# In the last two context blocks a pair's zero-point terms are written while the pair in front of it is multiplied

## The chip, the cores and the metric

The kernel runs on one core of one Trainium2 chip. The metric is the device time of one execution in microseconds, the median of several runs. The engines are called as the profile calls them: PE (TensorE, matmuls), PEld (its weight loads), ACT (ScalarE), DVE (VectorE), POOL (GpSimd) and SP (SyncE, which issues most DMAs).

## The reference

Two layers are computed for x (2 x 1024 x 2048) and a context ctx (2 x 2048 x 2048), all in float32. The first is a quantised product with the context, the second a feed-forward product with low-rank additions:

```python
def fake_quant(x, scale, zp):
    q = jnp.clip(jnp.round(x / s + z), 0.0, 255.0)
    return (q - z) * s
x = x + matmul(fake_quant(layernorm(x), x1_scale, x1_zp), fake_quant(ctx, x2_scale, x2_zp))
z = layernorm(x)                      # seen as 8 groups of 256 rows, one gate row each
delta = B_eff(gate) @ (A_eff(gate) @ z) + B_shared @ (A_shared @ z)
x = x + z @ kernel + bias + delta     # A_eff, B_eff: gated sums over 16 low-rank pairs
```

## The kernel before

**Batches, groups and blocks.** The two batches b run one after the other. The 1024 rows of a batch are four groups g of 256 rows, each of which is two tiles of 128 rows, j = 0 and 1. The 2048 columns of the context are four blocks n of 512. The quantised rows (`c1T`, less 128) and the quantised context block (`c2`, less 128) are small whole numbers and are multiplied in bf16. What is still missing from the product because the zero point is not 128 is added as two terms: `colt[n]`, a row of 512 values that belongs to the block, and `r_s`, a value for each row.

**A pair.** One group with one block is a `Pair` (line 513). Its accumulator `pa` is a tile of two PSUM banks, one for each j. Three such tiles, with the tags acc0, acc1 and delta, are used in turn, so that a pair takes the tile of the pair three before it. For each j, `begin(j)` (line 523) lets ScalarE write `colt + r_s` into the bank, and `products(j, ...)` (line 528) adds 16 matmuls of 128x128 by 128x512 to it. Then `end()` (line 545) lets VectorE scale both banks and add them to y, and `stats()` (line 549) takes the statistics for the second layer norm. `late(j)` (line 540) adds the terms afterwards instead; three early pairs of batch 0 use it.

**The order of the pairs.** In batch 0 all pairs of blocks 0 and 1, and pair (n=2, g=0), run in `entry()` by the list `STEPS`, an order written out by hand, which also keeps VectorE, ScalarE and PE in that order. The rest of batch 0, and all pairs of batch 1, go through `xattn_pair` (line 555). Pairs are named (n, g) below. The loops that call it for the last two blocks are those of lines 1056 and 1071. Beside the pairs of block 2 they round and centre block 3 of the context (`quantise`, lines 458 and 464), make the gated sums of the first low-rank factor (`lora_a_step`, line 593: matmuls of line 574 into `pg_a`, a copy of line 590, transposes of line 600, copies of line 606) and then block 3's column term (`column_term`, line 474: matmuls of lines 486 and 505, and line 511 that writes `colt`). Beside the pairs of block 3 they make the gated sums of the second factor (`lora_b_step`, line 611: line 574 into `pg_b`, a copy of line 590, and small DMAs of line 616 on SP's queue), load the first weights of the feed-forward part, and normalise and transpose each group that is complete (`group_z`, line 635: VectorE's line 628, PE's transposes of line 632 into `ptz`, ScalarE's copies of line 633). After pair (3,2) and group 1 `lora_ax` (line 642) multiplies the first two groups with the low-rank factor (`px`, line 648), and VectorE adds the halves of two groups (line 1093), two of them into buffers that a gated sum has read. The feed-forward products follow (line 828, `fu`, `fv`, `fw`), a scheme with seven products of sums of quarters (lines 31 to 50), whose operands VectorE and GpSimd combine (lines 762 and 771).

**Rows prepared between pairs.** In batch 0 all row tiles are prepared in `entry()`. In batch 1 the tiles of groups 0 and 1 are prepared during the feed-forward part of batch 0, and those of groups 2 and 3 (tiles 4 to 7) between the pairs of blocks 0 and 1, by the loop of lines 1036 to 1041: `prep_x` for both tiles of a group, then the group's pairs with blocks 0 and 1. The preparation (`prep_x`, line 436) takes VectorE's statistics, ScalarE's rounding of the row (line 409), and then for each half of the row ScalarE's centring with a running sum (line 412), eight transposes on PE (line 423) and VectorE's copy into `c1T` (line 428). At the end VectorE makes the tile's `r_s` from the two sums (line 432). The centred half rows have one buffer each (`qh`, two halves in the scratch tile `wk`), which all row tiles share, so a tile's line 412 follows the transposes of the tile before it.

**What sets the order.** Outside `entry()`, the order of the instructions on each engine is worked out when the kernel is built, from a model of their durations: of the instructions whose inputs the model says are there, the one that was written first in the program goes first. `tc.high_priority()` puts what it encloses in front of others that are ready. On the chip each engine then works through its list in that order, and waits where an input is late.

In `xattn_pair` the begin of the second half is written behind the products of the first half:

```python
for j in range(MG):
    with tc.high_priority():
        p.begin(j)
    p.products(j, range(KT))
```

Of the kernel before, what the change touches and what calls it, by code (L numbers as in the profile page):

```python
# [98 lines left out]
def tile_quant_xattn_then_lora_ffn(  # L99
# [27 lines left out]
    GPB = GB // B  # L127
    GT = B * S // GB
    MG = GT // P
# [38 lines left out]
    def bf(t, n):  # L168

        return t.rearrange("p k n -> p (k n)").bitcast(BF16).rearrange("p (k n) -> p k n", n=n)  # L170
# [280 lines left out]
    def quantise(c2, r):  # L451

        centre_ctx(c2, r, round_ctx())
# [20 lines left out]
    def column_term(b, n, c2):  # L474

        of = column_parts(b, n, c2)
        column_copy(of)
        column_mean(b, n, of)
        column_end(n, of)
# [72 lines left out]
                    st2[:, self.g * MG + j, self.n, :], y[self.g][:, j, ds(self.n * NB, NB)]  # L552
                )

    def xattn_pair(b, n, g, c1T, c2):
        p = Pair(b, n, g, c1T, c2)
        for j in range(MG):
            with tc.high_priority():
                p.begin(j)
            p.products(j, range(KT))  # L560
        summed = p.end()
        p.stats()
        return summed
# [29 lines left out]
    def lora_a_step(b, n):  # L593

        lora_a_place(n, lora_a_turn(b, n, *gated(f"a{b}_{n}")))
# [15 lines left out]
    def lora_b_step(b, n):  # L611

        st, sf = gated(f"b{b}_{n}")
        for c in range(NC):
            for i in range(2):
                nc.sync.dma_start(
                    out=bd[b][i::2, i, ds(c * RC, RC), ds(n * NB, NB)],
                    in_=sf[ds(c * GP + i * (GP // 2), GP // 2), :],
                )
        q2b.give(st)  # L620
# [14 lines left out]
    def group_z(b, g, wk, zq):  # L635
        for j in range(MG):
            prep_z(b, g * MG + j, zq, wk)
        for q in range(4):
            nc.scalar.dma_start(out=zs[b][g][q], in_=zq[q])
        return zq  # L640

    def lora_ax(b, pr, zqs):

        px = ps_m.tile([P, GT], F32, tag="pm", name=f"px_{b}_{pr}")
        for k in range(KT):
            for i in range(2):
                g = 2 * pr + i
                nc.tensor.matmul(  # L648
                    px[i * 2 * R : (i + 1) * 2 * R, :],
                    acat[:, k, ds(3 * pr + i, 2), :].rearrange("p s r -> p (s r)"),  # L650
                    zqs[i][k // KQ][:, k % KQ, :],
                    start=(k == 0),
                    stop=(k == KT - 1),
                    skip_group_check=True,
                )
        nc.scalar.copy(axT[:, pr, :], px)
# [245 lines left out]
    c1T = [bf(t, GT) for t in c1T_bufs]  # L902
    wk = big.take()
    c2b = {}
    c2 = {}
# [114 lines left out]
    for b in range(B):  # L1020
        if b == 0:
            open_c2(0)
            open_c2(1)
            with in_order(mybir.EngineType.DVE, mybir.EngineType.Activation, mybir.EngineType.PE):
                opened, begun = entry()
            next_block(1)
            with tc.issue_after(last_of[mybir.EngineType.DVE]):
                for p in begun.values():
                    p.stats()
        else:  # L1030
            gate_matrix(b)
            opened = xattn_pair(b, 0, 0, c1T, c2[0])
            xattn_pair(b, 0, 1, c1T, c2[0])
            for g in range(2):
                xattn_pair(b, 1, g, c1T, c2[1])
            for g in range(2, GPB):
                for m in range(g * MG, (g + 1) * MG):
                    with tc.issue_after(opened.ins):
                        prep_x(b, m, c1T, wk)
                for n in range(2):  # L1040
                    xattn_pair(b, n, g, c1T, c2[n])
                    if g + 1 == GPB:
                        next_block(n)
                        if n == 0:
                            for r in range(NR):
                                quantise(c2[2], r)
                                if r % 4 == 3:
                                    lora_a_step(b, r // 4)
                            column_term(b, 2, c2[2])
# [5 lines left out]
                    nc.sync.dma_start(out=bd[bb][g, 1 - g % 2], in_=b_sh)  # L1055
        for g in range(GPB):
            if (b, g) != (0, 0):
                xattn_pair(b, 2, g, c1T, c2[2])
            for r in {0: range(3), 1: range(3, 6), 2: range(6, 8), 3: ()}[g]:
                quantise(c2[3], r)  # L1060
            if 1 <= g <= 2:
                lora_a_step(b, g + 1)
            if g == 2:
                column_term(b, 3, c2[3])
# [4 lines left out]
        first.load("b11")  # L1069
        zqs = {}  # L1070
        for g in range(GPB):
            xattn_pair(b, 3, g, c1T, c2[3])
            big.give(c1T_bufs[g])
            if g == 0:
                first.block("b11")
                first.load("b12")
            elif g == 1:
                first.block("b12")
                first.comb("t1", "b12", "b11", ALU.subtract)
            elif g == 2:  # L1080
                first.load("b22")
            if g < 3:
                lora_b_step(b, g + 1)
            if g > 0:
                zqs[g - 1] = [lit.take() for _ in range(4)]
                group_z(b, g - 1, wk, zqs[g - 1])
            if g == 2:

                lora_ax(b, 0, [zqs[0], zqs[1]])
                for i in range(2):  # L1090
                    for j in range(2):
                        to = lit.take() if i == 0 else zqs[i][j]
                        nc.vector.tensor_add(to, zqs[i][j], zqs[i][2 + j])
                        first.t[f"a{i + 1}{j + 1}"] = to
                for t in (*zqs[0], *zqs[1][2:]):
                    lit.give(t)
# [72 lines left out]
        if b + 1 < B:  # L1169
            c1T_bufs, c1T, wk = state["c1b"], state["c1T"], state["wk"]  # L1170
# [53 lines left out]
```

## Time and profile before

| | |
|---|---|
| Median of 3 runs | 1082.38 us (1082.28 to 1082.62) |
| The profiled execution | 1082.56 us |
| Its span in the profile | 1080.8 us |
| Granted PE clock | 1.00 |
| Matmuls of the pairs (line 530) | 1024, median 379 ns each, one every 0.22 us |
| Begins (line 526) | 58, median 691 ns |
| Batch 0, rest of blocks 2 and 3 | about 102 to 180 us |
| Batch 1, blocks 0 and 1 | about 557 to 626 us |
| Batch 1, blocks 2 and 3 | about 626 to 708 us |

A line of the timeline gives the start and the length in microseconds, the engine, the source line, the operation, what it writes and reads, the shapes, and how many were merged into the line. In brackets stands how long the engine had been idle before it, and whose end released it. A matmul's listed length is longer than its share of PE, since matmuls overlap. The chain of waits is followed back from the last instruction, at each step to what released it. In the list of a source line, "its engine sat idle before it" names who released it, with the sum in microseconds and the count.

### The profile page before, as it was taken

How to read it: one execution, taken by the hardware profiler on the slowest of the kernel's cores; microseconds unless marked ns; L12 is line 12 of the kernel's file. 1: busy time of each engine (PE TensorE's matmuls, PEld its weight loads, DVE VectorE, ACT ScalarE, POOL GpSimd, SP SyncE). 2: the span in 40 equal slices, each digit the busy share in tenths (PEclk: the TensorE clock that was granted, in tenths of full speed). 3: DMA queues.
4: the chain of work that ended last, by engine and by line, in shares of the span. 5: the costliest groups of instructions: out<-in, count | busy, mean ns of one | idle time of the engine just before them, and what ended most of it. 6: DMA issues, size and time to landing. Idle time of an engine off the chain costs nothing.

```text
span 1080.8 us, 10609 instructions
## 1 busy us (share of the span) xinstructions
PE 1054.6 (98%) x3932; PEld 489.8 (45%) x3932; DVE 766.6 (71%) x949; ACT 247.4 (23%) x351; POOL 253.8 (23%) x104
## 2 busy tenths in 40 slices
PE   5999999999999999999999999999999999999998
PEld 2443345544444444444444444554444444444443
DVE  7986867578877676677859655674969667756851
ACT  5866133210000000001675741331000000000000
POOL 0000003032435302533000000032244531253600
PEclk9999999999999999999999999999999999999999
DMA  9979645788798476699673292559889874748611
GB/s 341 381 196 308 190 176 190 256 316 295 263 339 324 160 264 217 191 372 321 230 246 119 98 266 103 198 210 360 294 269 297 288 269 148 264 146 301 214 39 58
DMA packets 119228, 257.15 MB, mean 238 GB/s; under 512 B 11272, under 2 KB 15496, under 8 KB 118152
## 3 DMA queue, kind: packets, MB, share of 16 engines
q1 hardware_dynamic: 98688, 215.05, 58.4%
q10 hardware_dynamic: 20168, 40.38, 10.7%
q0 software_dynamic: 320, 1.05, 0.4%
q8 instruction: 31, 0.51, 0.2%
q14 instruction: 21, 0.17, 0.1%
HBM read 220.79 MB, written 37.75 MB: 239 GB/s over the span
## 4 chain that ended last, share of the span: by engine, by line
PE 83%; DVE 8%; DMA 4%; ACT 3%; issue 1%; SPq 0%; ACTq 0%
PE fu L828 34%; PE fv L828 17%; PE pa L530 12%; PE fw L828 9%; PE pl L694 3%; PE px L648 3%; PE ptz L632 2%; DMA lit<-in_ctx_dram 2%; DVE st L551 2%; DVE st L383 1%; ACT q2b L458 1%; DVE y L547 1%; ACT big L412 1%; DVE big L771 1%; PE pg_b L574 1%
## 5 line engine op out<-in xcount | busy, mean ns | idle before, releaser
L828 PE MATMUL fu<-big,lit 128*128 128x512 f32 x896 | 395.3, 593 | 0.0
L828 PEld LDWEIGHTS fu<-big,lit 128*128 128x128 f32 x896 | 168.6, 190 | 206.3 <-issue 204.9
L530 PE MATMUL pa<-big,big 128*128 128x512 bf16 x1024 | 237.1, 381 | 7.3 <-ACT pa L526 3.4
L771 POOL TENSOR_TENSOR lit<-lit,lit 128x1024 f32<-128x1024 f32 x56 | 164.7, 2950 | 189.7 <-PE fw L828 74.6
L828 PE MATMUL fv<-big,lit 128*128 128x512 f32 x448 | 197.9, 594 | 0.0
L771 DVE TENSOR_TENSOR big<-big,big 128x2048 f32<-128x2048 f32 x56 | 164.4, 2935 | 0.7
L530 PEld LDWEIGHTS <-big 128*128 128x128 bf16 x1024 | 97.1, 98 | 136.3 <-issue 29.6
L762 POOL TENSOR_TENSOR lit<-lit,lit 128x1024 f32<-128x1024 f32 x32 | 85.7, 2677 | 256.4 <-DMA lit<-zs 230.4
L852 DVE TENSOR_TENSOR y<-y,fu 128x1024 f32<-128x1024 f32 x92 | 108.5, 1215 | 40.6 <-PE fu L828 40.2
L828 PEld LDWEIGHTS fv<-big,lit 128*128 128x128 f32 x448 | 84.3, 190 | 105.0 <-issue 104.7
L458 ACT ACTIVATE q2b<-lit,sc,inv 128x1024 int16<-128x1024 f32 x64 | 76.4, 1232 | 163.7 <-DMA lit<-in_ctx_dram 147.1
L852 DVE TENSOR_TENSOR y<-y,fv 128x1024 f32<-128x1024 f32 x48 | 56.8, 1218 | 78.8 <-PE fv L828 78.8
L762 DVE TENSOR_TENSOR big<-big,big 128x2048 f32<-128x2048 f32 x40 | 101.8, 2546 | 0.0
L828 PE MATMUL fw<-big,lit 128*128 128x512 f32 x224 | 99.4, 592 | 0.0
L683 ACT COPY pl<-bias 128x1024 f32<-128x1024 f32 x16 | 16.3, 1018 | 294.1 <-DVE y L705 258.1
L679 POOL DMA_DIRECT2D bp<-bd x4 | 2.6, 660 | 344.3 <-DMA bd<-q2b 166.3
L852 DVE TENSOR_TENSOR y<-y,fw 128x1024 f32<-128x1024 f32 x24 | 28.4, 1218 | 53.9 <-PE fw L828 53.9
L828 PEld LDWEIGHTS fw<-big,lit 128*128 128x128 f32 x224 | 42.1, 190 | 50.7 <-issue 50.7
L547 DVE SCALAR_TENSOR_TENSOR y<-pa,k_s,y 128x1024 f32<-128x1024 f32 x32 | 41.0, 1280 | 32.2 <-PE pa L530 32.1
L526 ACT ACTIVATE pa<-bp,r_s 128x512 f32<-128x512 f32 x58 | 39.0, 685 | 87.0 <-PE pa L530 57.1
L705 DVE TENSOR_TENSOR y<-pl,y 128x512 f32<-128x512 f32 x64 | 39.8, 679 | 17.5 <-PE pl L694 17.2
L383 DVE BATCH_NORM_STATS2 st<-y 128x6 f32<-128x512 f32 x64 | 41.4, 679 | 5.7 <-DMA y<-in_x_dram 5.6
(93 smaller groups left out, 629.6 us busy)
## 6 DMA issues: line engine op xcount, KB each, us to landing
big<-in_w_dram SPq DMA_DIRECT2D x96, 1024.0 KB
lit<-zs SPq DMA_DIRECT2D x80, 512.0 KB
lit<-in_ctx_dram SPq DMA_DIRECT2D x64, 512.0 KB
out_dram<-y ACTq DMA_DIRECT2D x30, 512.0 KB
zs<-lit ACTq DMA_DIRECT2D x24, 512.0 KB
lit<-in_lora_a_dram SPq DMA_DIRECT2D x32, 256.0 KB
lit<-in_lora_bt_dram SPq DMA_DIRECT2D x32, 256.0 KB
y<-in_x_dram SPq DMA_DIRECT2D x16, 512.0 KB
```

Of the source, the lines that this page charges most:

```text
L383: nc.vector.bn_stats(st1[:, self.m, n, :], self.y[:, ds(n * NB, NB)])
L458: nc.scalar.activation(qi, t, AF.Relu, bias=z2, scale=inv2)
L526: nc.scalar.activation(self.pa[:, j, :], colt[self.n], AF.Identity, bias=r_s[:, m : m + 1])
L530: nc.tensor.matmul(self.pa[:, j, :], self.c1T[:, k, ds(j * P, P)], self.c2[k // 8][:, k % 8, :], start=not self.begun[j], stop=(k == KT - ...
L547: return nc.vector.scalar_tensor_tensor(yp, self.pa, s12, yp, ALU.mult, ALU.add)
L648: nc.tensor.matmul(px[i * 2 * R : (i + 1) * 2 * R, :], acat[:, k, ds(3 * pr + i, 2), :].rearrange("p s r -> p (s r)"), zqs[i][k // KQ][:, ...
L694: nc.tensor.matmul(pl[j][i][:, half], axT[rows, pr, ds(j * P, P)], bt[rows, half], start=False, stop=True, skip_group_check=True,)
L705: line(nc.vector.tensor_add(yb, pl[j][i], yb))
L762: line(eng.tensor_tensor(got[0], got[0], got[1], ALU.add if terms[1][2] > 0 else ALU.subtract))
L771: line(eng.tensor_tensor(out_t, at[p], at[q], op))
L828: nc.tensor.matmul(ps[m], at[:, k, ds(m * P, P)], bt[:, k, :], start=(opens and k == 0), stop=(ends and k == KQ - 1), skip_group_check=True,)
L852: line(nc.vector.tensor_tensor(yp, yp, whole[chain], op))
```

## The change

`xattn_pair` is split. `begin_pair` takes the accumulator of a pair and writes both its begins at once, with high priority. `xattn_pair` takes a pair that has been begun, or begins it on the spot, then begins the pair named by a new argument `then`, and only after that writes the pair's own products, its end and its statistics. The two loops over the last two context blocks, in both batches, name the next pair: the next group of the same block, or after the last group of block 2 the first of block 3. After the last pair of block 3 nothing is named. The other calls of `xattn_pair` (blocks 0 and 1 of batch 1) name nothing; there both begins of a pair now stand ahead of its products.

```diff
-    def xattn_pair(b, n, g, c1T, c2):
-        p = Pair(b, n, g, c1T, c2)
+    ready = {}
+
+    def begin_pair(b, n, g, c1T, c2):
+        p = ready[b, n, g] = Pair(b, n, g, c1T, c2)
+        with tc.high_priority():
+            for j in range(MG):
+                p.begin(j)
+
+    def xattn_pair(b, n, g, c1T, c2, then=None):
+        if (b, n, g) not in ready:
+            begin_pair(b, n, g, c1T, c2)
+        p = ready.pop((b, n, g))
+        if then:
+            begin_pair(b, *then)
         for j in range(MG):
-            with tc.high_priority():
-                p.begin(j)
             p.products(j, range(KT))
         summed = p.end()
         p.stats()
...
             if (b, g) != (0, 0):
-                xattn_pair(b, 2, g, c1T, c2[2])
+                xattn_pair(b, 2, g, c1T, c2[2], (2, g + 1, c1T, c2[2]) if g + 1 < GPB else (3, 0, c1T, c2[3]))
...
         for g in range(GPB):
-            xattn_pair(b, 3, g, c1T, c2[3])
+            xattn_pair(b, 3, g, c1T, c2[3], (3, g + 1, c1T, c2[3]) if g + 1 < GPB else None)
```

## The prediction

> **What bounds the kernel now.** I read the page first, then the busy time by stage, then the two blocks that the change names, and at last the other place that calls the changed function: blocks 0 and 1 of batch 1.
>
> ```profile
> PE 1054.6 (98%) x3932; PEld 489.8 (45%) x3932; DVE 766.6 (71%) x949; ACT 247.4 (23%) x351; POOL 253.8 (23%) x104
> ```
>
> PE is busy for 1054.6 of 1080.8 us, so a gain is bounded by its idle time, and each new gap on it is paid in full. Busy time by stage (from, to and length, then PE):
>
> ```profile
> 180.00:215.00 35.00, 33.17 (x179) 19.16 (x178) 23.17 (x32) 10.35 (x21) 9.14 (x4) 1.00 0.65 226
> 590.00:612.00 22.00, 21.95 (x140) 10.69 (x139) 13.21 (x30) 14.34 (x21) 0.00 (x0) 1.00 0.00 1
> 640.00:708.00 68.00, 67.83 (x397) 32.98 (x396) 39.86 (x84) 16.58 (x33) 3.75 (x4) 1.00 0.54 184
> ```
>
> PE has gaps of 1.8 us behind the blocks of batch 0 (180 to 215), 0.05 in 590 to 612, and 0.2 in the last blocks of batch 1. The waits for begins (line 526) in the blocks that the change names are these, with the order on both engines:
>
> ```profile
> 108.30 11.03 PE L530 MATMUL pa<-big,big 128*128 128x512 bf16 x50 [0.63 <-ACT pa L526]
> 124.77 0.59 PE L530 MATMUL pa<-big,big 128*128 128x512 bf16 x2 [0.78 <-ACT pa L526]
> 131.79 3.63 PE L530 MATMUL pa<-big,big 128*128 128x512 bf16 x16
> 135.35 1.06 PE L574 MATMUL pg_b<-lit,gmat 128*32 128x512 f32 x8
> 163.37 1.02 PE L828 MATMUL fu<-big,lit 128*128 128x512 f32 x2
> ```
> ```profile
> 135.46 0.69 ACT L526 ACTIVATE pa<-bp,r_s 128x512 f32<-128x512 f32 x1 [2.54 <-PE pa L530]
> ```
>
> Counting 32 products a pair back from the last, 131.79 is the first half of pair (3,0). It ends at 135.42, and the begin of the second half starts at 135.46, released by it, though the halves lie in different PSUM banks: order is kept for the whole accumulator tile. PE mostly steps around the blocked half with other due work (a gated sum at 135.35). Only 0.63 and 0.78 us, and 0.23 in batch 1 (631.39), found none.
>
> Now batch 1, where rows of groups 2 and 3 are prepared between pairs:
>
> ```profile
> 591.10 0.62 PE L423 MATMUL pt<-ident_h,big 128*128 128x128 bf16 x8
> 591.56 0.81 PE L530 MATMUL pa<-big,big 128*128 128x512 bf16 x3
> 592.24 0.62 PE L423 MATMUL pt<-ident_h,big 128*128 128x128 bf16 x8
> ...
> 606.63 1.67 PE L530 MATMUL pa<-big,big 128*128 128x512 bf16 x7
> 608.15 0.61 PE L423 MATMUL pt<-ident_h,big 128*128 128x128 bf16 x8
> 608.59 2.11 PE L530 MATMUL pa<-big,big 128*128 128x512 bf16 x9
> ```
> ```profile
> 594.08 0.27 DVE L432 TENSOR_SCALAR r_s<-rsum,k_s 128x1 f32<-128x1 f32 x1
> ...
> 610.39 0.26 DVE L432 TENSOR_SCALAR r_s<-rsum,k_s 128x1 f32<-128x1 f32 x1
> ```
>
> The second begin of (0,2) needs the `r_s` of row tile 5, there at 594.35; that of (0,3) needs row tile 7's, 610.65. But PE multiplies the first half of (0,2) from 590.17 (4, 3 and 9 products) and that of (0,3) from 606.63 (7 and 9), before those exist and while the second tile's rows are still being transposed (line 423). These halves are what fills PE there.
>
> **The change part by part.** No instruction is added or removed; begins move, and the order is worked out anew.
>
> *Waits removed.* 0.63 + 0.78 in batch 0, 0.23 in batch 1: 1.64.
>
> *Small waits added.* In the named blocks a pair's first products also wait for the second begin, which the pair in front covers, except at block 2's first pair. In batch 0 the begins start at 102.01 and 102.62, so PE resumes 0.62 later. In batch 1 (625.44 on) the same would be up to 0.45, but PE arrives later by the next item: 0.
>
> *Rows that come too late.* `xattn_pair` now writes both begins ahead of all products in every call. If order holds for the whole tile, (0,2)'s first product waits until row tile 5 is finished. Transposes of row tile 4 (585.02, 586.15) fill the blocked half of (1,1) now; with no such gap they follow (1,1). That pair ends at 590.2 less their 0.9 (two of 0.44), about 589.3, and they end at 590.1. ScalarE's two halves of line 412 for tile 5 share one buffer with tile 4, so they run 589.75 to 592.0 (1.13 each); the last transposes end at 592.6, placing takes 0.7, the sum 0.27, the begin 0.7: 594.3. PE has 0.9 of transposes for the 4.2 us from 590.1: **3.3 idle**. At (0,3): (0,2) and (1,2) are 64 products of 0.22, from 594.3 to 608.4. Tile 6's transposes come behind them (609.3), tile 7's line 412 from 609.0 to 611.3, transposes 611.8, place and sum 612.7, begin 613.4. PE has 0.9 of transposes and the gated sum (1.0, now at 610.63; its data are there, as the DMAs stand still in 590 to 612) for 4.1: **2.2 idle**. Together 5.5, all on the path, since PE is full from there to 708.
>
> Bounds: the trace shows the tile-wise wait for a begin behind products, not for products behind the other half's begin. If that doesn't exist, 0. If the transposes of tiles 4 and 6 slip in early as now, (0,2) waits from 590.2 for a begin that could end at 592.9 (sums done at 592.18, plus 0.7): 2.7 less 0.9, and (0,3) nothing, so 1.8. If the present chain stays and nothing fills: begins end at 595.1, 4.1 idle, and 3.2 at (0,3), so 7.3. I take 5.5: an order kept for a tile has no direction.
>
> [...]
>
> *Work that moves.* Gated sums (1.0 us each at 135.35, 143.36, 155.45) fall behind their pairs: the same PE time. SyncE's small writes behind them move too; PE first reads that scratch at 201.5. At 163.37 two FFN products (0.86) fill the gap in (3,3). The chain of waits leaves PE at that pair's end, goes through VectorE, and comes back with the transposes:
>
> ```profile
> 178.51 0.98 PE pa L530 x4
> ...
> 195.30 1.06 PE ptz L632 x8
> ```
>
> PE stands 1.72 us in front of 195.30. The two products now fall into that gap: -0.86 (bounds 0 and -1.72). In batch 1 the like gap is 0.24 (713.53): -0.24.
>
> *ScalarE's queue.* At block 2's start in batch 0 four begins are ready instead of two, ahead of the rounding at 103.24: 1.24 late at worst, and through VectorE's full 108 to 125 us so is block 3's column term. Its begins would end at 132.1 (now 130.28, plus one begin, plus 1.24), while PE has work to 131.0: at most 1.1. At best VectorE ends (2,0) first. I take 0, as another gated sum (1.0) can fill.
>
> *Sum.* Batch 0: -1.41 + 0.62 - 0.86 = -1.65. Batch 1: 5.5 - 0.23 - 0.24 = 5.03. Together +3.4. The profiled execution took 1082.56 (span 1080.8 and 1.8 around it), 0.18 over the median of 1082.38; from the median: **1085.8**. What is late next is PE itself: everything behind 594 in batch 1 shifts.
>
> **The rivals.**
>
> *The rows are hidden (1082.1).* One mechanism on the other side: PE's new order keeps the transposes of tiles 4 and 6 inside (1,1) and (1,2), so tile 7 is ready before PE comes to it and tile 5 costs 1.8. Then +1.8 - 1.65 - 0.47 = -0.3: 1082.1. It decides at 2.1 us of row waits, below which the kernel isn't slower. For it: now 8 and 5 transposes run inside those pairs. Against: there they fill halves that were blocked, and the pairs are written earlier in the program, so they go first when ready.
>
> *Begins and products don't meet (1079.6).* If products don't wait for the other half's begin, neither the 5.5 nor the 0.62 is paid: -1.65 - 0.62 - 0.47 = -2.7. Against it stands 135.46.
>
> *More is lost (1088.7).* Nothing fills (7.3) and the column term is late (1.1): -1.65 + 1.1 - 0.47 + 7.3 = +6.3.
>
> *It does nothing.* First begins already run ahead and PE already finds fillers: 1082.4. This holds for the named blocks almost as it is, not for the rows.
>
> **How the numbers follow.** 0.2% (2.2 us) is what a measurement of this kernel can tell from no change. The sum, with 1084 to 1088 around it, has 0.62; hidden rows, or nothing, 0.22; no meeting 0.08; more lost 0.08. About 0.05 of the sum's chance lies below +2.2, so slower by over 0.2% is 0.66, within 0.2% 0.25, faster 0.09. The range reaches from 1081.3, inside the hidden rows, to 1088.3.
>
> **What would show it.** Right: PE idle of 2 to 4 us at (0,2) near 592 and at (0,3) near 611, released by L526; no product of (0,2) or (0,3) before row tile 5 or 7 has its L432; second begins directly behind first ones in the last blocks, and no PE wait for them there but at block 2's start. Wrong: PE full in 585 to 615, transposes of line 423 inside (1,1) and (1,2), or first-half products ahead of the second begin; then the result lies at or below the time of before.

## The result, and the profile after

The changed kernel takes 1100.37 us (median of 4 runs, 1095.35 to 1101.27), the kernel before, measured beside it, 1082.50 us: a ratio of 1.0155, 95% interval 1.0124 to 1.0186. The forecast was 1085.8 us with a range from 1081.3 to 1088.3; the sign was right and the size far too small. The profiled execution took 1101.27 us with a span of 1099.5, so 18.7 us are to be found.

The page's first line of engines:

```profile
PE 1058.1 (96%) x3902; PEld 495.0 (45%) x3932; DVE 774.3 (70%) x949; ACT 247.8 (23%) x351; POOL 249.0 (23%) x104
```

PE's work is the same (30 of its records are missing here, which count as idle time), but it stands 41.4 us instead of 26.2, and it is busy longer for the same work. The busy time by stage, with the granted clock as the third number from the end:

```profile
180.00:215.00 35.00, 33.97 (x174) 20.79 (x176) 20.19 (x31) 10.59 (x21) 2.70 (x2) 0.91 0.55 195
590.00:612.00 22.00, 18.16 (x108) 9.94 (x107) 13.11 (x34) 18.48 (x26) 0.00 (x0) 0.84 0.01 1
640.00:708.00 68.00, 67.33 (x343) 29.73 (x351) 35.84 (x71) 15.44 (x26) 0.56 (x1) 0.97 0.58 175
```

The clock was 1.00 in all three stages before. Here it is 0.91, 0.84 and 0.97: PE ran at half clock for 6.83 us from 179.8, 6.83 us from 596.2 and 3.41 us from 640.6. The prediction has no term for that.

Now the timeline of PE where the last two blocks of batch 0 end:

```profile
131.95 13.99 PE L530 MATMUL pa<-big,big 128*128 128x512 bf16 x62
...
166.49 7.13 PE L658 MATMUL px<-lit,acat 128*64 128x256 f32 x64
173.78 3.83 PE L530 MATMUL pa<-big,big 128*128 128x512 bf16 x17 [0.16 <-issue]
181.03 1.94 PE L642 MATMUL ptz<-ident,big 128*128 128x128 f32 x8 [3.42 <-DVE big L638]
```

The change does what it says. 62 products run without a wait for a begin, and the two waits of 0.63 and 0.78 us are gone. But the order around them is a new one: `px` stands ahead of the last 17 products of (3,3), and no feed-forward product is left between these and group 2's transposes. PE stands 3.42 us, up to 181.03, and from 179.8 on the clock is 0.50.

Blocks 0 and 1 of batch 1:

```profile
592.88 1.06 PE L423 MATMUL pt<-ident_h,big 128*128 128x128 bf16 x16
597.00 2.17 PE L423 MATMUL pt<-ident_h,big 128*128 128x128 bf16 x16 [3.07 <-ACT big L412]
...
601.48 0.63 PE L530 MATMUL pa<-big,big 128*128 128x512 bf16 x1
```

Between (1,1), which ends at 593, and the first product of (0,2) at 601.48 PE has only transposes, and waits 3.07 us for ScalarE's rows: ScalarE rounds two tiles (line 409, 4.06 us from 591.75) before it centres tile 5 (line 412, from 595.72). At (0,3), where the transposes of tile 7 run from 616.08, it waits for nothing.

At (0,0), the first pair of batch 1, PE waits 1.02 us and then another 0.71 (at 562.40) in front of matmuls of a column term. In the kernel before it multiplied the first half of (0,0) meanwhile (from 557.01).

```profile
561.29 0.40 PE L486 MATMUL pcp<-big,ones_h 128*32 128x512 bf16 x4 [1.02 <-DVE big L428]
```

At the start of block 2 in batch 1, first the kernel before and then the changed one:

```profile
637.10 1.07 PE L574 MATMUL pg_a<-lit,gmat 128*32 128x512 f32 x8
```
```profile
633.59 2.54 PE L530 MATMUL pa<-big,big 128*128 128x512 bf16 x11
640.12 1.52 PE L584 MATMUL pg_a<-lit,gmat 128*32 128x512 f32 x8 [4.00 <-DMA lit<-in_lora_a_dram]
```

The gated sum `pg_a`, which stood inside (2,1) before, was put ahead of (2,0) and waits 4.00 us for its load.

**The account of the 18.7 us**, idle time of the changed kernel (called after) less that of the kernel before: the begins' waits -1.41 and -0.23; block 2's first pair in batch 0 1.67 - 1.36 = +0.31; group 2's transposes in batch 0 3.42 - 1.72 = +1.70; (0,0) 1.02 + 0.71 = +1.73; (0,2) 3.07 + 0.26 + 0.19 - 0.51 = +3.01; the load +4.00; the transposes of batch 1 near 730, 2.05 + 1.55 - 0.24 = +3.36. That is 12.5. In the three stretches of half clock (17.07 us) PE was busy for 14.3 us; if this work takes half the time at full clock (eight transposes into `ptz` took 1.94 us at 181.03 and 1.04 at 735.92), they cost 7.1. The sum is 19.6, 0.9 more than was to be found; this difference is not placed.

### The profile page after: what moved, and what is told of

Read it like the earlier page. It is cut to its first block, busy times and chain, and to the rows that moved or that the text cites. A ratio compares the mean times of both kernels' runs of the same rounds, so it can differ in the third digit from the quotient of the medians.

```text
span 1099.5 us, 10579 instructions
## 1 busy us (share of the span) xinstructions
PE 1058.1 (96%) x3902; PEld 495.0 (45%) x3932; DVE 774.3 (70%) x949; ACT 247.8 (23%) x351; POOL 249.0 (23%) x104
## 4 chain that ended last, share of the span: by engine, by line
PE 85%; DVE 6%; DMA 4%; ACT 2%; issue 1%; SPq 0%; DVEq 0%; ACTq 0%
PE fu L838 34%; PE fv L838 17%; PE pa L530 15%; PE fw L838 9%; PE pl L704 3%; PE ptz L642 2%; PE px L658 2%; DMA lit<-in_ctx_dram 2%; DMA lit<-in_lora_a_dram 2%; ACT big L412 1%; DVE big L781 1%; DVE big L638 1%; PE pt L423 1%; PE pg_a L584 1%; ACT q2b L458 1%
## 5 line engine op out<-in xcount | busy, mean ns | idle before, releaser
L530 PE MATMUL pa<-big,big 128*128 128x512 bf16 x994 | 232.1, 383 | 8.2 <-DVE big L428 2.6
L781 POOL TENSOR_TENSOR lit<-lit,lit 128x1024 f32<-128x1024 f32 x56 | 165.3, 2961 | 187.5 <-PE fw L838 89.6
L772 POOL TENSOR_TENSOR lit<-lit,lit 128x1024 f32<-128x1024 f32 x32 | 80.5, 2516 | 266.8 <-DMA lit<-zs 223.2
L526 ACT ACTIVATE pa<-bp,r_s 128x512 f32<-128x512 f32 x58 | 38.2, 681 | 57.1 <-DVE bp L511 31.4
```

The lines of the kernel that those rows point to most:

```text
L526: nc.scalar.activation(self.pa[:, j, :], colt[self.n], AF.Identity, bias=r_s[:, m : m + 1])
L530: nc.tensor.matmul(self.pa[:, j, :], self.c1T[:, k, ds(j * P, P)], self.c2[k // 8][:, k % 8, :], start=not self.begun[j], stop=(k == KT - ...
L772: line(eng.tensor_tensor(got[0], got[0], got[1], ALU.add if terms[1][2] > 0 else ALU.subtract))
L781: line(eng.tensor_tensor(out_t, at[p], at[q], op))
```

## The experiments

Times in what follows are medians. The "company" of a run is the kernel before, measured beside it on the same chip; "look-ahead" means that the next pair's begins stand ahead of a pair's products. The kernel before ran at 1083.3 to 1084.2 us in the experiments' company (single runs between 1080.9 and 1086.5), and each result is read against it.

| run | us | before, same company | ratio (95%) |
|---|---|---|---|
| last_blocks | 1094.83 | 1083.49 | 1.0108 (1.0088 to 1.0127) |
| blocks01_order | 1093.31 | 1083.49 | 1.0084 (1.0064 to 1.0103) |
| ahead_batch0 | 1084.49 | 1083.49 | 1.0014 (0.9996 to 1.0033) |
| ahead_batch1 | 1093.40 | 1083.49 | 1.0091 (1.0067 to 1.0115) |
| graded_stalls | 1111.41 | 1084.22 | 1.0260 (1.0205 to 1.0316) |
| hold_gated | 1087.74 | 1084.22 | 1.0043 (1.0020 to 1.0066) |
| adds_on_vector | 1081.44 | 1084.22 | 0.9984 (0.9973 to 0.9995) |
| rows_first | 1093.37 | 1084.22 | 1.0091 (1.0070 to 1.0113) |
| turn_first | 1091.56 | 1083.37 | 1.0073 (1.0055 to 1.0092) |
| adds_only | 1084.24 | 1083.37 | 1.0011 (0.9998 to 1.0025) |
| adds_ahead0 | 1082.73 | 1083.37 | 0.9984 (0.9974 to 0.9994) |
| repaired_both | 1083.57 | 1083.37 | 1.0001 (0.9992 to 1.0010) |
| but_00_02 | 1087.71 | 1083.33 | 1.0045 (1.0027 to 1.0062) |
| only_00_02 | 1085.95 | 1083.33 | 1.0025 (1.0014 to 1.0037) |

### Which of the three places loses

Four kernels keep the order of before (begin, products, begin, products) wherever `ahead` is false:

```diff
     def xattn_pair(b, n, g, c1T, c2, then=None):
+        ahead = b in (0, 1) if n >= 2 else False   # last_blocks
+        # blocks01_order: b in () if n >= 2 else True
+        # ahead_batch0:   b in (0,) if n >= 2 else False
+        # ahead_batch1:   b in (1,) if n >= 2 else False
+        if not ahead:
+            p = Pair(b, n, g, c1T, c2)
+            for j in range(MG):
+                with tc.high_priority():
+                    p.begin(j)
+                p.products(j, range(KT))
...
```

> Pairs of blocks 0 and 1 in batch 1 keep the order of the kernel before (begin, products, begin, products); the look-ahead stays in the last two blocks of both batches. Theory (all three places lose): only the loss at (0,0) and (0,2) of batch 1, 8 us by the trace's milestones (+3.1 at the first column term, +11.3 at the first product of (0,2)), goes away: about 1092, between 1088 and 1094. Rival A (the loss is the late rows of blocks 0 and 1 and what follows from them, the wait of 4.00 us for the gated sum's load too): 1080 to 1083. Rival B (the look-ahead itself loses everything): 1099 to 1101.

> Only the pairs of blocks 0 and 1 of batch 1 have both begins ahead of the products; the last two blocks keep the order of the kernel before. Theory: a wait at (0,0) of about 1.7 us and one of about 3 us with a stretch of half clock (3.4 us lost) at (0,2): 1089 to 1092, granted clock 0.5 once near 595. Rival A: the same and the wait for the load behind it with a second stretch: 1094 to 1099. Rival B: 1082 to 1083.

> Look-ahead in the last two blocks of batch 0 alone; all of batch 1 keeps the order of the kernel before. Theory: the idle of 3.4 us in front of the transposes of group 2 and the half clock behind it stay: 1085 to 1086. Rival A (batch 0 gains its 0.63 and 0.78, and the 3.4 us belong to a chance of timing): 1080.5 to 1082.5. Rival B: more than 1090.

> Look-ahead in the last two blocks of batch 1 alone; everything else keeps the order of the kernel before. Theory: the gated sum that is put ahead of (2,0) waits 2 to 4 us for its load also with rows that are on time, and one stretch of half clock follows if the wait is over 3 us: 1085 to 1090. Rival A (that wait came from the late rows): 1081.5 to 1083. Rival B: over 1090.

Measured against before: last_blocks +11.3, blocks01_order +9.8, ahead_batch0 +1.0, ahead_batch1 +9.9. The two batches' look-aheads add up (1.0 + 9.9 = 10.9 for 11.3); with the 9.8 of blocks 0 and 1 the sum is 20.7, 2.8 more than the 17.9 of the change, so the parts aren't quite independent. So blocks 0 and 1, which the change meant to leave alone, and the look-ahead of batch 1 lose about the same, batch 0 hardly anything (1.0 here, not clear of noise, where the account of the profiled execution gave it about 3.4), and rival A (late rows alone) and rival B (the look-ahead alone) both fall as an account of the whole. last_blocks lies 0.8 above its theory's range and ahead_batch0 0.5 under its own. blocks01_order lies 1.3 above the theory's range: a wait of 2.12 us for a begin at block 2's start and a second stretch of half clock come on top (the mean granted clock of that execution is 0.997). ahead_batch1 lies 3.4 above its range: the wait for the load is followed by two stretches of half clock (6.83 us from 631.2; 63 products from 634.15 took 15.88 us, 13.97 in hold_gated) and not one, and 2.05 us of standing in front of the transposes near 721 cost a third (3.41 us from 723.34). There the rows are on time, and the load is waited for all the same:

```profile
632.14 2.08 PE L594 MATMUL pg_a<-lit,gmat 128*32 128x512 f32 x8 [5.13 <-DMA lit<-in_lora_a_dram]
```

So this wait isn't a consequence of late rows. ahead_batch0 spread from 1082.20 to 1091.39 with one and the same program, which asked for the next experiment.

### What a gap costs in clock

Six calls of this function are put into the written-out order of batch 0, and nothing is left out:

```diff
+        def stall(n, w):
+            to, j = recent[-1]
+            f = axT.rearrange("p a t -> p (a t)")[:, 0 : 128 * w]
+            nc.scalar.activation(f, to[:, j, 0 : 128 * w], AF.Identity)
+            for i in range(n):
+                nc.scalar.activation(f, f, AF.Identity)
+            nc.scalar.activation(tick, f[:, 0:1], AF.Identity)
+            nc.tensor.matmul(to[:, j, :], zeros_h, tick.to_broadcast([P, NB]), start=False, stop=True, ...)
```

> The kernel before, with six waits put into batch 0 between 45 and 85 us: PE stands while ScalarE works off a short chain (of 2 to 6 activations), about 1.9, 2.3, 2.9, 3.0, 3.5 and 4.7 us long; nothing is left out. Theory (the clock is set for fixed stretches of 3.41 us by how long PE stood in the stretch before, with a limit near 2 us): half clock after the 4.7 and the 3.5 us, after the shorter ones only where 2 us or more of them fall into one stretch; time 1082.5 + 18 + 1.7 for each stretch at half clock, 1104 to 1112. Rival (the length of the gap alone decides, from 3.0 us): half clock after every gap of 3.0 us or more, after no shorter one. Rival (idle time has nothing to do with it): no half clock, 1100 to 1101.

The six gaps came out as 2.42, 2.11, 2.96, 3.09, 3.63 and 4.95 us (from 39.91, 48.12, 55.31, 65.39, 78.22 and 91.70). The half-clock stretches in the rows below began at 51.22, 58.04, 95.59 and 99.00 us, multiples of 3.41 us from one another. They show busy time in stretches cut on that grid; the number before the comma is their length, then come PE's busy time and, third from the end, the granted clock:

```profile
37.57:40.98 3.41, 2.34 (x11) 0.97 (x10) 3.01 (x12) 3.38 (x6) 0.00 (x0) 1.00 1.02 422
40.98:44.39 3.41, 2.06 (x10) 0.97 (x10) 2.06 (x4) 3.35 (x6) 0.00 (x0) 1.00 1.02 423
47.81:51.22 3.41, 1.30 (x5) 0.50 (x4) 1.01 (x2) 2.88 (x7) 0.00 (x0) 1.00 1.06 386
51.22:54.63 3.41, 3.41 (x15) 1.76 (x14) 2.93 (x6) 1.14 (x2) 0.00 (x0) 0.50 1.07 240
54.63:58.04 3.41, 0.68 (x3) 0.20 (x2) 0.09 (x1) 2.51 (x5) 0.00 (x0) 1.00 1.08 241
58.04:61.45 3.41, 3.17 (x8) 1.17 (x8) 2.35 (x7) 3.15 (x5) 0.00 (x0) 0.50 1.04 357
61.45:64.87 3.42, 3.42 (x17) 1.54 (x16) 3.31 (x6) 0.00 (x0) 0.00 (x0) 1.00 1.06 267
...
92.18:95.59 3.41, 0.00 (x0) 0.00 (x0) 0.00 (x0) 3.25 (x6) 0.00 (x0) 1.00 0.00 0
95.59:99.00 3.41, 2.14 (x5) 0.86 (x6) 1.70 (x4) 3.25 (x8) 0.00 (x0) 0.50 0.00 0
99.00:102.41 3.41, 3.41 (x17) 1.88 (x16) 2.22 (x14) 1.02 (x2) 0.00 (x0) 0.50 0.02 5
```

The gap of 2.42 us falls across the cut at 40.98 (1.07 before it and 1.35 behind it), and the stretch from 40.98 runs at 1.00, like that from 47.81. The shorter gap of 2.11 lies inside one stretch, and the next stretch runs at 0.50. After the gap of 4.95 PE also stood 1.27 us inside the half-clock stretch, and the one behind it stayed at half. So the length of a gap alone doesn't decide; the rival with a limit of 3.0 us falls, and so does the one without any effect. The median of only two runs, 1111.4, lies in the theory's range, the profiled run (1116.27) above it; later waits stand in it too (1.81 us at 133.3, 1.53 at 618.0). In after, 1.67 us of standing in a full-clock stretch left the clock at 1.00 (101.27) and 2.17 did not (176.37); nor did 2.05 in ahead_batch1 (719.93). The cuts fall elsewhere in each profile (at 101.27 in after and 102.41 in graded_stalls, at 725.93 in after and 726.75 in ahead_batch1), so it is luck what a gap of 2 to 3 us costs: no half clock in these rows for the 2.42, one stretch for the 2.11. That fits a part of ahead_batch0's spread, whose only long gap in the profile is 3.07 us; how its slower runs went isn't known.

### The gated sum that waits for its load

```diff
             if 1 <= g <= 2:
-                lora_a_step(b, g + 1)
+                with tc.issue_after(held.ins) if b == 1 else nullcontext():   # held: (2,g)'s last product
+                    lora_a_step(b, g + 1)
```

> Look-ahead in the last two blocks of batch 1 alone, as in ahead_batch1, but there the gated sums of the last two column blocks stand on PE behind the last product of their pair. Theory (the sum is pulled ahead of its load): the wait of 5.1 us and the half clock behind it go, 1.7 to 3.4 us more; the 2.05 us in front of the transposes near 721 stay: 1083 to 1087. Rival (the loads come that late for another reason, and whoever stands next waits): 1089 to 1093.

```profile
627.59 13.97 PE L530 MATMUL pa<-big,big 128*128 128x512 bf16 x63 [0.97 <-ACT pa L526]
641.49 1.07 PE L595 MATMUL pg_a<-lit,gmat 128*32 128x512 f32 x8
```

The wait is gone: (2,0) and (2,1) run through, and the sum finds its data at 641.49. The loss against before falls from 9.9 us (ahead_batch1) to 3.5; 1087.74 lies 0.7 above the expected range. The 2.05 and 1.55 us in front of the transposes near 715 stay. The load was never late: it landed at 632.1 in ahead_batch1, and the order of before simply asked for it later, at 637.1.

### Why the transposes wait

In after, these are the steps of VectorE that group 2's transposes wait for in batch 0, and GpSimd beside them:

```profile
173.23 2.53 DVE L349 SCALAR_TENSOR_TENSOR nt_z<-ve_z,r_z 128x1 f32<-128x1 f32 x2
...
175.87 2.26 DVE L358 TENSOR_TENSOR rstd_z<-r_z,nt_z 128x1 f32<-128x1 f32 x2
178.09 3.52 DVE L638 TENSOR_SCALAR big<-y,mv_z,rstd_z 128x1024 f32<-128x1024 f32 x2
```
```profile
173.26 7.07 POOL L781 TENSOR_TENSOR lit<-lit,lit 128x1024 f32<-128x1024 f32 x3 [1.95 <-DVE r_z L347]
```

Two operations on one value a partition take 2.53 us, where the same pair takes 0.35 in adds_on_vector (174.63). Each time the first of the two lasts until a GpSimd sum of 2.35 us ends (175.63 against 175.61, 178.05 against 178.04), and the first operation of the last line, 2.79 us long, ends 0.55 us behind the third sum. That GpSimd's sums hold up VectorE's steps is inferred from these rows. The test takes the sums off GpSimd:

```diff
             eng, pool = (nc.gpsimd, lit) if p[0] in "as" else (nc.vector, big)
+            if (self.b, self.o) == (0, 0) and name in ("s1", "s2", "s3"):
+                eng = nc.vector
```

> Look-ahead in the last two blocks of batch 0 alone, as in ahead_batch0, but the first three sums of quarters (s1, s2, s3), which GpSimd makes while VectorE normalises group 2, are made by VectorE. Theory (GpSimd's additions hold up VectorE's small steps): these steps take 0.2 us instead of 2.2 to 2.8, the 3.1 us idle in front of the transposes of group 2 falls below 1, the granted clock stays 1.0 in batch 0: 1080.5 to 1082.5. Rival (the statistics of group 2 come late because of the order on ScalarE and VectorE): idle stays at 2.5 to 4 us, 1083 to 1087.

```profile
174.63 0.35 DVE L349 SCALAR_TENSOR_TENSOR nt_z<-ve_z,r_z 128x1 f32<-128x1 f32 x2
...
175.28 1.53 DVE L648 TENSOR_SCALAR big<-y,mv_z,rstd_z 128x1024 f32<-128x1024 f32 x2
```

PE takes group 2's transposes right behind (3,3), at 178.86, with no idle time, and the kernel is faster than before (0.9984, 0.9973 to 0.9995). So the 3.1 us of ahead_batch0 were GpSimd's sums, not the order of the statistics. Two more kernels ask who earned the gain:

> The kernel before with the first three sums of quarters of batch 0 on VectorE instead of GpSimd, no look-ahead anywhere. If the look-ahead brings what adds_on_vector gained in batch 0 (0.63 and 0.78 us of waits): no change against before, within 0.5 us, and 1 to 2 us slower than adds_on_vector. If moving the sums brings it: 1 to 2 us under before, equal to adds_on_vector.

> The kernel of adds_on_vector once more, in the same company: look-ahead in the last two blocks of batch 0 and the first three sums on VectorE. If the look-ahead gains there: 1 to 2 us under adds_only, 1080.5 to 1082. If not: equal to adds_only within 0.5 us.

adds_only has the same three lines on the kernel before, adds_ahead0 is the kernel of adds_on_vector again. adds_only is no faster than before (1.0011, 0.9998 to 1.0025); adds_ahead0 is, again by 0.16%, and its median is 1.5 us under that of adds_only, though at 1082.73 it lies 0.7 above its range. The rows of 0.63 and 0.78 us stand in the profile of adds_only and not in that of adds_ahead0. So in batch 0 the look-ahead does gain them, once nothing eats them. This is the version that beats both kernels.

### The rows of blocks 0 and 1

```diff
-        with tc.high_priority() if b == 0 else nullcontext():            # rows_first
+        with tc.high_priority() if b == 0 or m >= 4 else nullcontext():
             x.variance()
...
-            x.turn(h)                                                    # turn_first
+            with tc.high_priority() if m >= 4 else nullcontext():
+                x.turn(h)
```

> Both begins ahead of the products in blocks 0 and 1 of batch 1 alone, as in blocks01_order, but the rounding of row tiles 4 to 7 has high priority, so that rows are ready earlier. Theory (the second begin of (0,2) waits for late rows): the 2.5 us near 592 and the half clock behind them go, the 1.7 us at (0,0) stay: 1084 to 1087. Rival (the order of begins and products costs it whatever the rows do): 1090 to 1094.

> Both begins ahead of the products in blocks 0 and 1 of batch 1 alone, as in blocks01_order, but the transposes of row tiles 4 to 7 have high priority, so that those of tile 4 stand inside pair (1,1) again. Theory (the chain is: transposes of tile 4 behind (1,1), then the shared half-row buffer, then tile 5's rows, its r_s and the second begin of (0,2)): the 2.5 us in front of tile 5's transposes fall below 1, no half clock near 595: 1085 to 1089, as the 1.7 us at (0,0) and the waits at block 2 stay. Rival (the rows of tile 5 are late for another reason): 2 to 3 us idle stay there, 1091 to 1094.

Both missed, and the rivals' ranges held. rows_first keeps 2.88 us at the same place: a rounding (2.08 us from 591.08) stands ahead of tile 5's centring there too. turn_first does bring the transposes of tile 4 back into (1,1) (583.75 and 584.88), and still:

```profile
587.74 4.06 ACT L409 ACTIVATE big<-y,ox,kx 128x2048 uint8<-128x2048 f32 x2
591.72 1.13 ACT L412 ACTIVATE big<-big,n_centre 128x1024 bf16<-128x1024 uint8 x1
```
```profile
592.99 0.62 PE L423 MATMUL pt<-ident_h,big 128*128 128x128 bf16 x8 [2.96 <-ACT big L412]
```

The shared half-row buffer is free at 585.5, but ScalarE rounds tiles 5 and 6 one after the other (line 409, 4.06 us) before it centres tile 5. In before, one of these roundings stood there and the centring began at 589.82. So the prediction's chain (transposes, buffer, rows) holds in before's order, not in the new one. And even in before the centring ended only at 592, when PE, here free at 590, would have had nothing either: what filled that hole was the first half of (0,2).

Is it then those two pairs alone whose first halves are PE's only work?

> Both begins ahead of the products in blocks 0 and 1 of batch 1, except at (0,0) and (0,2), which keep begin, products, begin, products; the last two blocks as before. Theory (the loss of blocks01_order sits where a pair's first half was PE's only work, at (0,0) and (0,2)): no idle over 1 us between 555 and 615, clock 1.0 there, 1082.5 to 1085. Rival (every pair with both begins ahead takes work away from PE, and the 1.8 to 2.1 us at block 2 come from that order too): 1086 to 1091.

> Both begins ahead of the products at (0,0) and (0,2) of batch 1 alone; all else as before. Theory: 1 to 1.7 us idle at (0,0), 2.5 to 3.5 us at (0,2) and one or two stretches of half clock near 595: 1087 to 1091. Rival (it needs the other pairs' order too): 1083 to 1085.

The edit sets `ahead` to `n < 2 and (n, g) not in ((0, 0), (0, 2))`, and to `(n, g) in ((0, 0), (0, 2))`. The answer is no. only_00_02 costs 2.6 us (1.02 us idle at (0,0), 1.82 at (0,2)), under its range and above its rival's; but_00_02 costs 4.4, above its own and in its rival's: 1.56 us near 589, 1.30 + 1.18 us at (0,3), where 12 of tile 6's 16 transposes now stand behind (1,2) and hold up tile 7, and a stretch of half clock behind these (3.41 us from 610.7; the gated sum at 610.75 took 2.03 us, the one at 620.83 1.06). Together they make 7.0 of the 9.8. So the loss doesn't sit in those two pairs alone: the other pairs lose with the new order too, and the two losses don't make up the whole. Where the rest comes from wasn't traced; that PE still steps into first halves in each of the two kernels, and is offered none in blocks01_order, would fit.

### Everything repaired

repaired_both has the look-ahead in the last blocks of both batches, before's order in blocks 0 and 1, hold_gated's edit, and the sums of both batches on VectorE.

> Look-ahead in the last two blocks of both batches, blocks 0 and 1 of batch 1 in the order of before, the gated sums of batch 1 held behind their pair, the first three sums of quarters of each batch on VectorE. Theory (load, GpSimd and late rows are all that the look-ahead lost): no idle over 1.5 us after 110 us, clock 1.0 throughout, 1080 to 1082. Rival (the look-ahead costs something of its own at the end of batch 1): 1083 to 1087.

```profile
180.00:215.00 35.00, 34.94 (x179) 20.13 (x178) 24.18 (x34) 9.31 (x19) 2.36 (x1) 1.00 0.70 247
590.00:612.00 22.00, 21.84 (x138) 10.74 (x139) 13.31 (x31) 13.94 (x21) 0.00 (x0) 1.00 0.00 1
```

Both stages are full again at clock 1.00, and the time is that of before (1.0001, 0.9992 to 1.0010). So with the three causes, late rows, the early gated sum and GpSimd's sums, the loss against before is gone. The idle time and the clock are as the theory said, but the time isn't: it lies 1.6 us above the theory's range and in the rival's (the look-ahead costs something of its own). Block 2 of batch 1 now starts with a wait of 0.97 us (0.23 before), and the rest was not followed up, so that rival stands for a loss of this size.

## Why the prediction was wrong

The steps that failed are those on the work around the pairs. The prediction let it fall where PE has room (-1.1 for fillers, 0 for the gated sums); it cost 9.1 us (1.70 + 3.36 + 4.00). The half clock behind three of the long gaps, 7.1 us, had no term. Item by item:

- **The waits removed** (1.64): right, place by place.
- **Small waits added** (0.62): 0.31 in the profile. This wait at block 2's start is between 0.81 and 2.25 us in the profiles with before's order there, and between 0.93 and 2.33 in those with the look-ahead, so the term can't be tested more closely.
- **ScalarE's queue** (0): right. At the start of block 3 in batch 0 PE runs from 131.95 without a wait for a begin.
- **Rows that come too late** (5.5): right in its first half. Order is kept for the whole accumulator in both directions, and no first half runs ahead of the second begin (in rows_first, below, the second begin of (0,2) ended at 599.28 and the first product started at 599.33). That (0,2) stands 3.0 us, where 3.3 were predicted, is partly luck: the chain to tile 5's rows was to go through the shared buffer, and went through two roundings on ScalarE (4.06 us), so PE waited for line 412 and not, as predicted, for L526. (0,3) was predicted at 2.2 and stood for nothing, since tile 6's transposes (599.43, 600.65) ran inside (0,2)'s hole and tile 7 was early; in but_00_02, where that hole is shorter, a wait of 2.5 is there. (0,0) was left out of the sum, though it is the same edit: its second begin now stands on ScalarE behind a rounding of 1.23 us and another pair's begin, and its first half is what PE did meanwhile. It costs 1.73. The three places together make 4.7 for the 5.5, but not where the sum had them.

```profile
559.40 0.69 ACT L526 ACTIVATE pa<-bp,r_s 128x512 f32<-128x512 f32 x1 [0.99 <-DVE bp L511]
560.03 1.23 ACT L458 ACTIVATE q2b<-lit,sc,inv 128x1024 int16<-128x1024 f32 x1
561.16 1.28 ACT L526 ACTIVATE pa<-bp,r_s 128x512 f32<-128x512 f32 x2
```

- **Work that moves** (-0.86 and -0.24): this step failed. It took the order around the pairs as that of before, with the fillers falling where they were wanted. The order is worked out from modelled times, and the new one put `px` ahead of (3,3)'s end and no filler behind it, while VectorE's steps ran into GpSimd's sums; that the model has no term for this is inferred. Instead of -1.1 it cost 1.70 + 3.36.
- **The gated sums** (0, "the same PE time"): failed too. That the data are there was looked up for one sum only; the next one was pulled ahead of its load, +4.00.
- **The clock**: no term. Three gaps of 3.07 to 4.00 us cost 7.1 us more in half clock, the largest single item of the loss. The longest gap of before behind its first 20 us is 1.72 us (195.30), so its trace showed clock 1.00 and no price for a longer one.
- **The rivals**: "more is lost" had the right sign and 6.3 us, a third of it; "begins and products don't meet" is refuted. In rows_first the two begins of (0,2) are far apart. The begins that needed only tile 4's `r_s`, that of the first bank among them, had ended by 591.05; the second begin ended at 599.28. The first product, which goes into the first bank, waited for the second begin, so this program's semaphores keep order for the tile:

```profile
599.33 0.59 PE L530 MATMUL pa<-big,big 128*128 128x512 bf16 x1 [1.39 <-ACT pa L526]
```

## What to carry to other kernels

An edit of order has no neutral part where a list scheduler works out the rest: every caller of the changed function, every filler that stood in the old gaps and every load that was just in time has to be costed in the new order, not the old. A wait at which PE finds other work is cheap, and removing it can take the filler (the other work) from a dearer one. Where PE is nearly full, as here, a gap of more than about 2 us should be priced with a stretch of half clock behind it: 2.05 us inside one stretch brought 3.41 us of it (ahead_batch1, 719.93), 2.11 brought 3.41 (graded_stalls, 47.81) and 2.17 brought 6.83 (after, 176.37).

## What the runs showed of the hardware

In these traces PE's clock changed on a grid of 3.41 us: in after at 179.78, 186.61, 596.21, 603.03, 640.58, 643.99 and 1097.97, in graded_stalls at multiples of 3.41 us from 51.22. With 2.05 us (ahead_batch1, 719.93), 2.11 (graded_stalls, 47.81) or 2.17 (after, 176.37) of standing in one full-clock stretch the next ran at 0.50, with 1.67 (after, 101.27) it ran at 1.00; the gap of 2.42 across a cut in graded_stalls (40.98), 1.07 and 1.35 us on its two sides, left the stretch behind that cut at 1.00. Behind a half-clock stretch with 0.41 us of standing the next was full (after, 599.62), behind one with 1.15 it was half again (after, 596.21). In after, three GpSimd sums of 2.34 to 2.35 us stood beside three VectorE steps of 2.40, 2.19 and 2.79 us; most of the same steps there take 0.21, 0.15 and 0.81, and with the sums on VectorE their pairs take 0.35, 0.28 and 1.53 (adds_on_vector, 174.63 to 175.28).
